# Products by zero weights, a longer share for ScalarE and eight banks in a four-layer network kernel

## The chip, the cores and the metric

The kernel runs on one core of a Trainium2 chip. The metric is the device time of one execution in microseconds. Before the change it is 7317.06 us, the median of three runs (7311.98 to 7319.36).

A core has a matrix engine (TensorE, PE in the profile; its weight loads are PEld), a vector engine (VectorE, DVE), an activation engine (ScalarE, ACT), a general one (GpSimd, POOL) and a queue engine that here issues nearly all DMAs (SyncE, SP). Each engine works through its own instruction stream in order; they meet through semaphores. TensorE writes its sums to PSUM, which has eight banks of 128 x 512 fp32.

## The reference

The input x has shape (16, 32, 128, 128). Four layers follow each other, each x = x + f(normalised x):

1. a row recurrence: `g = xt + W1_prev·shift(h) + W1_cur·h + b`, gates by sigmoid and tanh, 128 steps;
2. an 8-bit difference layer over 3x3 patches of 32 channels: `out = -sum |patch - w|`, with quantised x and w. This is the one the change mostly concerns: 288 differences for each output of each of 32 channels;
3. a Hartley transform of which 32 x 32 modes are mixed over channels and transformed back;
4. a small U-shaped network: five fixed edge operators, each normalised, then conv1, pool, conv2, pool, conv3, pool, conv4, then three times an upsampling deconvolution and a convolution (conv5, conv6, conv7), and `x * y`.

## The kernel before

**First stage** (`stage0`): statistics and the recurrence, up to about 880 us. The change doesn't touch it.

**The unit loop** (`Differences.run`): layer 2. A unit is half an image: 16 images, two halves, 32 units. Partitions hold four row blocks of 32 channels (for the evaluations, four copies: four output channels of a group by 32 input channels). `|a - w|` is written as `2·max(a - w, 0) - (a - w)`; the second part is linear and done by TensorE alone (`linear`, L601, nine taps). For the first, a unit has 72 evaluations, i = 0 to 71: tap i % 9 of output channels 4·(i // 9) to +3. An evaluation reads the tile q (66 rows of 130, fp16) and writes a tile d of 128 x 8192 or 8320 fp16. It is made either by VectorE (L684, `d_dve`, three buffers) or by ScalarE as a Relu with bias (L681, `d_act`, two buffers). TensorE then adds each tile over input channels into the unit's four banks `acc1`: `sums` (L586), 16 products of 128 x 512 with a 128 x 32 weight (`sel16`), each of which sums into one 32-partition block of a bank. After 72 tiles `finish` evicts the banks on VectorE (L567, then statistics, L569) and stores x2. The four banks are the only ones of this pool, so the next unit's sums cannot begin before L567 has emptied them.

**The account.** The order of everything in the loop is written out by the kernel when it is built. It keeps an account with a time for each engine (`weave.dve`, `weave.act`, `weave.pe`), with fixed prices: `DVE_US = 2.36` for an evaluation on VectorE, `ACT_US = 7.15` on ScalarE, `PE_US = 1.0` for a tile's sums. It gives an evaluation to ScalarE where by the account this ends no more than 0.5 us after VectorE would (and not from i = 68 on), and it takes the tiles' sums in the order in which the tiles end. All sums of a unit, those of ScalarE's last tiles too, stand before the next unit's first evaluation. When two VectorE tiles of the next unit stand in the order, the old unit's `finish` follows and the new banks are taken.

**The interleaved work** (`After`, a generator). Layers 3 and 4 of images already finished, in groups of four images: group 0 to 2 in a `Weave`. After each evaluation `weave.advance(due)` takes steps of this work as long as the account has TensorE free before the next tile ends. Its stages are `forward` (L1030), `mixing` (L1096), `back` (L1159, L1204, evicted by L1182, L1184), `statistics` (L1292), `conv1` (L1607), the small layers (L1455 for conv2 to conv4, L822 and L847 for the composed upsampling convolutions) and `last` (L822, L1735, L1698, L1708, store L1714). It has four banks of its own (pool `b_ps`). `spread` (L1543 on VectorE, L1546 on ScalarE) moves results with a bias, 16 pieces at a time, to the next padded tile.

**The tail** (`drain`). When the loop ends, the four `acc1` banks are given to a second weave, `end`, for group 3 alone (pool `c_ps`). `drain` takes steps of both weaves by turns, by their accounts, until both are done. In the profile the tail begins at 5942 us; group 2's last stores are issued at 7048, and from then group 3 is alone with its four banks.

Of the kernel before, what the change touches and what calls it, by code (L numbers as in the profile page):

```python
# [7 lines left out]
F32 = mybir.dt.float32  # L8
F16 = mybir.dt.float16
# [6 lines left out]
B, C, H, W = 16, 32, 128, 128  # L16
# [283 lines left out]
class Weave:  # L300
# [10 lines left out]
    def __init__(self, work):  # L311
        self.work, self.pending = work, None
        self.pe = self.dve = self.act = self.now = self.base = 0.0
        self.until = self.ready = 0.0
        self.draining = False
        self.finished, self.count, self.put_off, self.for_act, self.ends = -1, 0, [], [], {}

    def later(self, us, step):
# [19 lines left out]
    def run(self, v):  # L338
        (self.put_off if v in self.put_off else self.for_act).remove(v)
        dve, act = self.dve, self.act  # L340
        v[2]()
        self.ends[v[1]] = max([t for t, before in ((self.dve, dve), (self.act, act)) if t > before] + [0.0])
# [60 lines left out]
def drain(*weaves):  # L403

    live = list(weaves)
    for w in live:
        w.draining = True
    while live:
        w = min(live, key=lambda w: w.now)
        us = w.step()  # L410
        w.now = max(w.now + (us or 0.0), w.until)
        w.due(float("inf") if us is None else w.now)
        if us is None:
            live.remove(w)


def keep_order(nc, tc, start):
# [13 lines left out]


DVE_US, ACT_US, PE_US = 2.36, 7.15, 1.0
SLACK, CLOCK = 3.0, 1.0
SUMMED = ("summed",)


def rest(nc, tc, cst, sel16, bias, m1, r1, a, d, out):


    with ExitStack() as ctx:
        sm = ctx.enter_context(tc.tile_pool(name="s1_sm", bufs=1))
        stat = sm.tile([128, B, 8, 6], F32, name="stat2")
        with tc.tile_pool(name="s1_ps0", bufs=2, space=PSUM) as ps:
            first = Differences(nc, sm, ps, cst, sel16, m1, r1, a["adder_w"], d, stat)
        bg = ctx.enter_context(tc.tile_pool(name="b_ps", bufs=4, space=PSUM))
        after = After(nc, tc, "left", sm, bg, cst, bias, a, d, stat, out)
        weave = after.weave = Weave(after.work(range(NG - 1)))
        start = len(nc.cur_bb.bb.instructions)
        with ExitStack() as front:  # L450
            first.run(tc, front, weave)
        keep_order(nc, tc, start)

        end = copy.copy(after)
        end.side, end.ps = "right", ctx.enter_context(tc.tile_pool(name="c_ps", bufs=4, space=PSUM))
        end.weave = Weave(end.work([NG - 1]))
        end.weave.now = end.weave.base = weave.now
        end.weave.finished = B - 1
        drain(weave, end.weave)


class Differences:
# [10 lines left out]
    def __init__(self, nc, sm, ps, cst, sel16, m1, r1, w, d, stat):  # L473
# [32 lines left out]
        for j in range(4):  # L506
# [4 lines left out]
                start=True,  # L511
# [2 lines left out]
        nc.vector.tensor_scalar(sumw, p[:, :1], 2.0**-7, None, ALU.mult)  # L514
        self.r128, self.shift, self.qw, self.neg, self.sumw = r128, shift, qw, neg, sumw

        self.ring = [sm.tile([128, 8, P], F16, name=f"qt{i}") for i in range(2)]
        for t in self.ring:
            nc.gpsimd.memset(t, 0.0)
# [40 lines left out]
            self.nc.sync.dma_start(xr[i], jc_rows(self.d["x1"], b, half, 8 * i, 8))  # L560
        return xr

    def finish(self, b, half, acc, xr):
        nc = self.nc
        v = [xr[k // 2][:, 512 * (k % 2) : 512 * (k % 2) + 512] for k in range(4)]
        for k in range(4):
            nc.vector.scalar_tensor_tensor(v[k], acc[k], self.sumw, v[k], ALU.subtract, ALU.add)  # L567
        for k in range(4):
            nc.vector.bn_stats(self.stat[:, b, 4 * half + k, :], v[k])  # L569

        def store():
            for i in range(2):
                nc.sync.dma_start(jc_rows(self.d["x2"], b, half, 8 * i, 8), xr[i])
            if half:
                self.weave.finished = b

        start = max(self.weave.dve, self.weave.pe)
        self.weave.pe, self.weave.dve = start + 2.6, start + 5.6
        self.weave.later(max(self.weave.dve - self.weave.base, 0.0) + 0.5, store)
# [14 lines left out]
    def linear(self, acc, q, tap):  # L594
# [12 lines left out]
                )  # L607
        self.weave.pe = max(self.weave.pe, self.weave.now) + 0.45

    def run(self, tc, ctx, weave):  # L610
        nc, R, P = self.nc, self.R, self.P
        self.weave = weave
# [5 lines left out]
        with tc.tile_pool(name="s1_x0", bufs=4, side="right") as pool:  # L618
            xq = [self.unquantised(0, i, pool) for i in range(4)]
            for i in range(4):  # L620
                self.scaled(0, xq[i])
                self.quantise(0, i, xq[i])
                weave.due(float("inf"))
        before, following = None, self.loaded(0, 0)

        free, count = {True: [0.0] * 2, False: [0.0] * 3}, {True: 0, False: 0}
        for b in range(B):
            for half in range(2):
                q, acc = following, None
                late, xq, summed = [], {}, 0  # L630

                def sums(until, last):

                    nonlocal summed
                    while late and (min(late)[0] <= until or last):
                        end, n, act, t = min(late)
                        late.remove((end, n, act, t))
                        self.sums(acc, t, n, not summed, last and not late)
                        summed += 1
                        weave.pe = max(weave.pe, end + 0.2) + PE_US  # L640
                        free[act].append(weave.pe)

                for i in range(72):
                    if not acc and sum(not v[2] for v in late) == 2:

                        if before:
                            self.finish(*before)
                        acc = [ps.tile([128, 512], F32, name="acc1") for _ in range(4)]
                        sums(weave.dve, False)
                    if i % 4 == 0 and 24 <= i < 60:  # L650
                        self.linear(acc, q, i // 4 - 6)
                    if i == 8 and (b, half) != (B - 1, 1):
                        following = self.loaded(b + half, 1 - half)
                    if i == 40:
                        xr = self.residual(b, half)
                    if half == 0 and b + 1 < B:
                        k = (i - 6) // 15
                        if 0 <= k < 4 and (i - 6) % 15 == 0:
# [11 lines left out]
                        for act in (True, False)  # L670
                        if count[act] < len(free[act])
                    }
                    act = False not in ends or (True in ends and i < 68 and ends[True] <= ends[False] + 0.5)
                    t = dp.tile([128, R, P], F16, name="d_act" if act else "d_dve", bufs=2 if act else 3)

                    src = q[:, kh : kh + R, :] if kw == 1 else q[:, kh : kh + R, kw : kw + W]
                    dst = t if kw == 1 else t[:, :, :W]
                    late.append((ends[act], i, act, t))
                    count[act] += 1
                    if act:  # L680
                        nc.scalar.activation(dst, src, AF.Relu, bias=self.neg[:, i : i + 1])  # L681
# [1 line left out]
                    else:  # L683
                        nc.vector.tensor_scalar(dst, src, self.qw[:, i : i + 1], 0.0, ALU.subtract, ALU.max)  # L684
                        weave.dve = ends[act]
                    if acc and (not act or i == 71):
                        sums(weave.dve, i == 71)
                    made = sum(not v[2] for v in late)
                    if acc:
                        weave.advance(min([v[0] for v in late] + [weave.dve + DVE_US]))  # L690
                    else:
                        weave.advance(weave.dve + (2 - made) * DVE_US + (2.6 if before else 0.0))
                before = b, half, acc, xr
        self.finish(*before)
        weave.due(float("inf"))


# [178 lines left out]
class After:  # L876


    def __init__(self, nc, tc, side, sm, ps, cst, bias, a, d, stat, out):
        self.nc, self.tc, self.side, self.ps, self.cst, self.bias = nc, tc, side, ps, cst, bias  # L880
        self.a, self.d, self.stat, self.out = a, d, stat, out
        store = [d["up"][i] for i in range(3)]
        self.up5 = Composed(nc, sm, a, "deconv1", "conv5", bias[:, 7:8], bias[:, 4:5], store[0])
        self.up6 = Composed(nc, sm, a, "deconv2", "conv6", bias[:, 8:9], bias[:, 5:6], store[1])
        self.up7 = Composed(nc, sm, a, "deconv3", "conv7", bias[:, 9:10], bias[:, 6:7], store[2])
# [16 lines left out]
                    yield from self.last(g)  # L902

    def acc(self):
        return self.ps.tile([128, 512], F32, name="acc")

    def prepare(self):

# [627 lines left out]
    def spread(self, dst, src, blk, b, engine):  # L1536

        nc, weave = self.nc, self.weave
        for j in range(4):
            d, s = dst(slice(32 * blk, 32 * blk + 32), j), src[32 * j : 32 * j + 32]  # L1540
            bj = b[32 * j : 32 * j + 32]
            if engine is nc.vector:
                nc.vector.tensor_scalar(d, s, bj, None, ALU.add)  # L1543
                weave.dve += 0.3
            else:
                nc.scalar.activation(d, s, AF.Identity, bias=bj)  # L1546
                weave.act += 0.45
# [115 lines left out]
    def last(self, g):  # L1663

        nc, tc, cst, weave = self.nc, self.tc, self.cst, self.weave
        with self.pool("l_y") as yp, self.pool("l_x", 2) as xp:
# [39 lines left out]
            def done(x, unit):  # L1706
                for blk in range(4):
                    nc.scalar.activation(x[:, blk], x[:, blk], AF.Identity, bias=mean[:, blk : blk + 1])  # L1708
                weave.act += 4.4
                following[unit] = weave.later(14.0, lambda: store(x, unit))  # L1710

            def store(x, unit):
                for j in range(4):
# [200 lines left out]
```

## Time and profile before

| what | value |
|---|---|
| median of three runs | 7317.06 us |
| the profiled execution | 7308.39 us, span 7306.6 |
| instructions | 258155 |
| first stage | 0 to 880 us |
| unit loop, first to last evaluation | 920 to 5942 us |
| evaluations on VectorE, ScalarE | 1705, 599 |
| tail, two groups | 5942 to about 7056 us |
| tail, group 3 alone | about 7056 to 7307 us |
| granted TensorE clock, mean | 0.867 |

```profile
PE 5566.3 (76%) x121132; PEld 3000.3 (41%) x121132; DVE 5855.4 (80%) x7046; ACT 5318.0 (73%) x3116; POOL 36.3 (0%) x31
...
PE   4778566666677687998777676999788777798887
...
DVE  7787599999999999999898889999899982423232
ACT  2556399989999998998988878999898941131312
...
PEclk9899788888888898998888887999887876799996
```

The first line gives busy time, share of the span and instructions of each engine. The rows below cut the span in 40 slices; a digit is the busy share in tenths, and PEclk is the clock that TensorE was granted, in tenths of full speed. Slices 6 to 32 are the unit loop.

### The profile page before, as it was taken

To read this page: it belongs to the slowest core of one execution; us is meant where nothing else is said; L and a number is where in the kernel's file an instruction comes from. 1 tells how busy PE (TensorE), PEld (TensorE's weight loads), DVE (VectorE), ACT (ScalarE), POOL (GpSimd) and SP (SyncE) were. 2 spreads that over 40 slices of the span, in tenths; PEclk is the share of its full clock that TensorE was granted. 3 is DMA by queue.
4 is the path that set the end of the run, shared out by engine and by line. 5 is a ranking of instruction groups with operands and counts; after the bars stand their busy time and mean duration, and the time that the engine had idled before them with its cause. 6 is when DMAs were issued, how large, how long until landed. Compare 5 with 4: busy or idle time off the path is not lost. (4 is left out here: it accounts for less than half of the span.)

```text
span 7306.6 us, 258155 instructions
## 1 busy us (share of the span) xinstructions
PE 5566.3 (76%) x121132; PEld 3000.3 (41%) x121132; DVE 5855.4 (80%) x7046; ACT 5318.0 (73%) x3116; POOL 36.3 (0%) x31
## 2 busy tenths in 40 slices
PE   4778566666677687998777676999788777798887
PEld 3665322222244343333344333333334456445544
DVE  7787599999999999999898889999899982423232
ACT  2556399989999998998988878999898941131312
POOL 0000000000000000000000000000000000000000
PEclk9899788888888898998888887999887876799996
DMA  8654111111133442211342243111233245531324
GB/s 312 227 195 164 65 63 55 48 58 51 40 96 106 136 115 78 62 43 50 78 134 94 79 139 111 58 55 50 57 100 100 98 138 151 156 102 46 81 62 96
DMA packets 374268, 721.67 MB, mean 99 GB/s; under 512 B 50896, under 2 KB 219856, under 8 KB 362320
## 3 DMA queue, kind: packets, MB, share of 16 engines
q1 hardware_dynamic: 372768, 704.58, 31.3%
q8 instruction: 948, 15.53, 0.9%
q14 instruction: 120, 0.98, 0.0%
q10 hardware_dynamic: 432, 0.57, 0.0%
HBM read 507.21 MB, written 164.32 MB: 92 GB/s over the span
## 5 line engine op out<-in xcount | busy, mean ns | idle before, releaser
L681 ACT ACTIVATE d_act<-q,neg 128x8192 f16<-128x8192 f16 (+1 forms) x599 | 4237.0, 7141 | 383.8 <-PE acc L586 330.8
L684 DVE TENSOR_SCALAR d_dve<-q,qw 128x8192 f16<-128x8192 f16 (+1 forms) x1705 | 3929.7, 2360 | 187.4 <-PE acc L586 144.1
L586 PE MATMUL acc<-d_dve,sel 128*32 128x512 f16 x27280 | 1957.5, 415 | 750.4 <-DVE d_dve L684 741.5
L586 PEld LDWEIGHTS <-sel 128*32 128x32 f16 x36864 | 1045.7, 103 | 2521.4 <-issue 1862.7
L1607 PE MATMUL acc<-xp,wf 32*32 32x512 f32 x25600 | 1052.9, 625 | 50.7 <-issue 29.9
L586 PE MATMUL acc<-d_act,sel 128*32 128x512 f16 x9584 | 759.4, 439 | 346.2 <-ACT d_act L681 276.9
L1607 PEld LDWEIGHTS acc<-xp,wf 32*32 32x32 f32 x25600 | 415.9, 105 | 428.5 <-issue 344.9
L1252 ACT ACTIVATE xp<-xp,shift,stats 128x1280 f32<-128x1280 f32 (+1 forms) x128 | 182.5, 1434 | 434.5 <-DMA xp<-x_d 298.3
L1546 ACT ACTIVATE y<-pooled,b 32x128 f32<-32x128 f32 x512 | 204.7, 400 | 398.8 <-DVE pooled L1532 392.1
L207 PE MATMUL pg<-h,wb 64*64 64x20 f32 (+15 forms) x4096 | 393.7, 318 | 105.0 <-DVE h L256 64.0
L822 PE MATMUL acc<-y,u_conv 32*32 32x256 f32 (+1 forms) x9728 | 409.9, 491 | 82.6 <-issue 41.0
L244 ACT ACTIVATE gt<-pg,bias 128x20 f32<-128x20 f32 (+15 forms) x1024 | 316.6, 375 | 78.8 <-PE pg L207 72.0
L207 PE MATMUL pg<-e,wb 64*64 64x20 f32 (+15 forms) x4096 | 351.1, 313 | 17.2 <-DVE e L260 6.0
L207 PEld LDWEIGHTS pg<-h,wb 64*64 64x64 f32 x4096 | 245.4, 152 | 140.9 <-DVE h L256 90.5
L207 PE MATMUL pg<-xn,wb 64*64 64x28 f32 (+61 forms) x4096 | 283.9, 302 | 11.6 <-ACT gt L244 3.9
L822 PEld LDWEIGHTS acc<-y,u_conv 32*32 32x32 f32 x9728 | 193.8, 115 | 233.3 <-issue 152.8
L207 PEld LDWEIGHTS pg<-e,wb 64*64 64x64 f32 x4096 | 249.3, 154 | 93.0 <-DVE e L260 63.9
L1292 PE MATMUL acc<-xp 32*64 32x204 f32 (+3 forms) x8576 | 245.6, 351 | 31.5 <-ACT xp L1258 23.4
L255 ACT ACTIVATE th<-c 128x20 f32<-128x20 f32 (+15 forms) x256 | 81.3, 320 | 236.1 <-DVE c L253 234.5
L1735 DVE TENSOR_SCALAR s<-acc,l_ms,l_one 128x512 f32<-128x512 f32 x128 | 102.7, 829 | 168.8 <-PE acc L822 168.8
L207 PEld LDWEIGHTS pg<-xn,wb 64*64 64x64 f32 x4096 | 216.0, 153 | 36.6 <-ACT gt L244 10.9
L1292 PEld LDWEIGHTS acc<-xp 32*64 32x64 f32 (+1 forms) x8576 | 173.3, 137 | 123.5 <-issue 93.3
(203 smaller groups left out, 4173.4 us busy)
## 6 DMA issues: line engine op xcount, KB each, us to landing
xr<-x_d SPq DMA_DIRECT2D x192, 512.0 KB
xp<-x_d SPq DMA_DIRECT2D x112, 640.0 KB
q<-q_d SPq DMA_DIRECT2D x32, 2145.0 KB
x_d<-xr SPq DMA_DIRECT2D x128, 512.0 KB
x_in<-in_x_dram SPq DMA_DIRECT2D x16, 2048.0 KB
res<-in_x_dram SPq DMA_DIRECT2D x64, 512.0 KB
xn<-in_xs_dram SPq DMA_DIRECT2D x64, 512.0 KB
xn<-xn SPq DMA_DIRECT2D x128, 256.0 KB
```

What stands on the lines that cost most here:

```text
L207: nc.tensor.matmul(bank[c][q][64 * pair : 64 * pair + 64, :, :width], wb[half, 4 * kind + KIND[q]].rearrange("p b o -> p (b o)"), v[half], ...
L244: nc.scalar.activation(gt[:, q, :, :n], bank[c][q][:, :, :n], AF.Tanh if q == G else AF.Sigmoid, bias=bias[:, KIND[q] : KIND[q] + 1],)
L255: nc.scalar.activation(th[:, :, :n], cell, AF.Tanh)
L586: self.nc.tensor.matmul(acc[k][32 * j : 32 * j + 32, :], self.sel16[:, i // 9, :], d[:, row : row + 4, c : c + W], start=first, stop=last,)
L681: nc.scalar.activation(dst, src, AF.Relu, bias=self.neg[:, i : i + 1])
L684: nc.vector.tensor_scalar(dst, src, self.qw[:, i : i + 1], 0.0, ALU.subtract, ALU.max)
L822: nc.tensor.matmul(acc[blk][32 * j : 32 * j + 32, o : o + rows * n], t[part, 4 * par + tap, :], src[part, top : top + rows, left : left + ...
L1252: nc.scalar.activation(v, v, AF.Identity, bias=self.shift3, scale=self.stats3[:, 1])
L1292: nc.tensor.matmul(gram[blk][j : j + width, at : at + n], xp[part, l, 2 + j : 2 + j + width], xp[part, rows, j : j + width + 4], start=sta ...
L1546: nc.scalar.activation(d, s, AF.Identity, bias=bj)
L1607: nc.tensor.matmul(acc[blk][32 * j : 32 * j + 32, :], tap_of("all", tap)[rows], xp[rows, 4 * j + kh : 4 * j + kh + 4, kw : kw + W], start= ...
L1735: nc.vector.tensor_scalar(s.rearrange("p r w b -> p b r w"), acc[blk].rearrange("p (b r w) -> p b r w", b=2, w=64), istd[:, blk : blk + 1] ...
```

## The change

Four things change.

- **Filler.** A tile `zero` of 128 x 32 zeros is added. After `advance`, where the account still has TensorE idle before the next tile ends, `keep_busy` issues up to four packets of four products with these weights, on rows of q, into the unit's own banks with accumulation: they add zero. A packet is put down as 0.25 us. Nothing is issued before a unit's first sum.
- **ScalarE up to a unit's end.** The limit i < 68 is replaced by a bound: in the last four evaluations ScalarE may take one that ends up to `(71 - i) * DVE_US + LATE` after VectorE's next would, `LATE = 1.5`. A unit's sums are now kept with the unit; those still open at its end are issued during the first evaluations of the next one, all of them ahead of `finish`.
- **Eight banks for the last group.** When one weave of the tail is done, the other is told that it is alone. From then `acc` takes banks by fours from its own pool and from the first weave's pool in turn.
- **Also when alone**, `spread` gives blocks 0 and 2 to VectorE and 1 and 3 to ScalarE instead of all to one of them, and the store of a finished unit of `last` is placed 4 us instead of 14 us of the account after its last step.

```diff
+LATE = 1.5
...
+        end.spare = bg
...
+        self.zero = sm.tile([128, 32], F16, name="zero")
+        nc.vector.memset(self.zero, 0.0)
...
+    def keep_busy(self, acc, q, until):
...
+        start = max(self.weave.pe, self.weave.now)
+        for k in range(min(int((until - start - 0.1) / 0.25), 4)):
+            for j in range(4):
+                self.nc.tensor.matmul(
+                    acc[k][32 * j : 32 * j + 32, :], self.zero, q[:, :4, :W], start=False, stop=False
+                )
+            self.weave.pe = start + 0.25 * (k + 1)
...
+        def sums(unit, until, last=False):
...
+            late = unit["late"]
+            while late and (min(late)[0] <= until or last):
+                end, n, act, t = min(late)
+                late.remove((end, n, act, t))
+                self.sums(unit["acc"], t, n, unit["summed"] == 0, unit["summed"] == 71)
+                unit["summed"] += 1
+                weave.pe = max(weave.pe, end + 0.2) + PE_US
+                free[act].append(weave.pe)
...
-                        if before:
-                            self.finish(*before)
+                        if before:
+                            sums(before, weave.dve, True)
+                            self.finish(**before)
...
-                    act = False not in ends or (True in ends and i < 68 and ends[True] <= ends[False] + 0.5)
+                    act = False not in ends or (
+                        True in ends and ends[True] <= ends[False] + (0.5 if i < 68 else (71 - i) * DVE_US + LATE)
+                    )
...
-                    if acc and (not act or i == 71):
-                        sums(weave.dve, i == 71)
-                    made = sum(not v[2] for v in late)
-                    if acc:
-                        weave.advance(min([v[0] for v in late] + [weave.dve + DVE_US]))
+                    current = unit if unit["acc"] else before
+                    if current and not act:
+                        sums(current, weave.dve)
+                    due = [v[0] for v in current["late"]] if current else []
+                    if unit["acc"]:
+                        due.append(weave.dve + DVE_US)
                     else:
-                        weave.advance(weave.dve + (2 - made) * DVE_US + (2.6 if before else 0.0))
+                        made = sum(not v[2] for v in unit["late"])
+                        due.append(weave.dve + (2 - made) * DVE_US + (2.6 if before else 0.0))
+                    weave.advance(min(due))
+                    if unit["acc"] and 0 < unit["summed"] < 71:
+                        self.keep_busy(unit["acc"], q, min(due))
...
     def acc(self):
-        return self.ps.tile([128, 512], F32, name="acc")
...
+        self.banks += 1
+        ps = self.spare if self.weave.alone and self.banks // 4 % 2 else self.ps
+        return ps.tile([128, 512], F32, name="acc")
...
-            if engine is nc.vector:
+            if blk % 2 == 0 if weave.alone else engine is nc.vector:
...
-                following[unit] = weave.later(14.0, lambda: store(x, unit))
+                following[unit] = weave.later(4.0 if weave.alone else 14.0, lambda: store(x, unit))
```

## The prediction

> **What bounds the kernel now.** I read the page first, then the busy time by stretches, the waits of each engine, a timeline of one unit's end, and the chain of waits for the end. The profiled execution took 7308.4 us (span 7306.6), 8.7 under the median of the runs, 7317.1; the sum is made on the profiled one and shifted by 8.7.
>
> ```profile
> L681 ACT ACTIVATE d_act<-q,neg 128x8192 f16<-128x8192 f16 (+1 forms) x599 | 4237.0, 7141 | 383.8 <-PE acc L586 330.8
> L684 DVE TENSOR_SCALAR d_dve<-q,qw 128x8192 f16<-128x8192 f16 (+1 forms) x1705 | 3929.7, 2360 | 187.4 <-PE acc L586 144.1
> ```
>
> The 2304 evaluations (32 units of 72) go to two engines. VectorE's overlap a little, so one costs its busy time over its count: 3929.7/1705 = 2.305 us. ScalarE's costs 7.14. These lines also show who waits: both for TensorE's sums (L586), ScalarE longer.
>
> ```profile
> 920.00:5942.00 5022.00, 3854.22 (x78058) 1799.89 (x78061) 4735.17 (x3735) 4588.63 (x1211) 28.82 (x15) 0.88 0.26 79
> 1100.00:2000.00 900.00, 579.00 (x8376) 237.16 (x8376) 892.39 (x705) 842.18 (x130) 6.34 (x2) 0.86 0.14 51
> 2900.00:3300.00 400.00, 389.23 (x8748) 147.38 (x8748) 381.94 (x256) 377.29 (x198) 0.21 (x1) 0.99 0.17 51
> ```
>
> Columns: length, then busy TensorE products, weight loads, VectorE, ScalarE, GpSimd, then TensorE's clock. The first row is the whole unit loop: VectorE idles 287 of 5022 us, ScalarE 433, TensorE 1168. VectorE sets the time, ScalarE is close behind. The second row is a stretch with little interleaved work: VectorE is 99% busy although the clock is 0.86. The third has much interleaved TensorE work: 97% busy, clock 0.99. So the clock follows TensorE's load, and where VectorE is full it costs nothing.
>
> ```profile
> DVE d_dve L684 <- PE acc L586: 144.1, 88, 26.7
> DVE d_dve L684 <- DMA q<-q_d: 41.2, 1, 41.2
> ...
> 1618.24 21.35 ACT L681 ACTIVATE d_act<-q,neg 128x8320 f16<-128x8320 f16 x3
> 1647.96 21.15 ACT L681 ACTIVATE d_act<-q,neg 128x8192 f16<-128x8192 f16 x3 [8.37 <-PE acc L586]
> ...
> 1644.46 2.72 DVE L567 SCALAR_TENSOR_TENSOR xr<-acc,sumw,xr 128x512 f32<-128x512 f32 x4
> ...
> 1645.26 4.30 PE L586 MATMUL acc<-d_act,sel 128*32 128x512 f16 x32 [3.29 <-DVE xr L567]
> ```
>
> First VectorE's waits (total, times, longest), then a unit's end. ScalarE's three evaluations from 1618 are the old unit's last and the new unit's first two. Both of its buffers are then full, and it stands 8.37 us until the old banks are evicted (L567) and its first new tile summed. Following its instructions through the units, 207 of the 330.8 us fall on this third evaluation of a unit, about 6.5 us a unit: nearly room for one more evaluation.
>
> **The change, part by part.**
>
> *ScalarE up to a unit's end.* The order built from the changed program has 622 ScalarE evaluations and 1682 on VectorE: 23 move. VectorE: 23 x 2.305 = **53 us** less, on the path. ScalarE: 23 x 7.14 = 164 us more, beside it: cover is the 207 us. Its loop load becomes 4589 + 164 = 4753; with the first load (47.8) and its waits for interleaved work (some 70) it could end the loop no earlier than 4871, 151 under today: the floor of the gain. VectorE's own floor is lower: 4735 - 53 + 41 = 4723, plus waits.
> The new wait: the old unit's last sum may now come from ScalarE after VectorE has gone on, and VectorE's eviction of the banks (L567), with the evaluations queued behind it, waits for it. In the trace ScalarE's last evaluation of a unit ends 7 to 21 us before VectorE's (mean about 14), so one more 7.1 us fits, less the 2.3 us that VectorE ends sooner; and VectorE has two evaluations of the next unit (4.6 us) ahead of the eviction. Per unit this costs between 0 and 3 us (ScalarE's account is true, VectorE's 2.36 is 0.055 too long, 2.9 us over 53 evaluations): 0 to 96 us. I take 10, by the mean slack.
>
> *Filler.* 7008 products, 1752 packets of four, in the form of L586 (128x512, f16, 32 columns). In the timeline two groups of sixteen start 0.86 us apart at full clock (1625.36, 1626.22) and 1.66 at half (3479.24, 3480.90), so four cost 0.21 or 0.42 us. At full clock that is 1752 x 0.21 = 370 us against 1168 idle, each packet put where the kernel's account leaves a gap. What does it buy? [...] The row: in 1100 to 2000 TensorE's waits for VectorE's tiles are 231.7 us in 201 (1.15 us each), and the clock is 0.86. [...] By the rows the share of busy time decides: cut into 3.4 us pieces, the clock record falls to 0.5 after pieces with under about 45% busy and returns after about 80%. The measurement decides: filler should lift the loop's clock from 0.88 to 0.95 or more. Whether products by zero count as load no row shows. Worth in time: at most all 144.1 us of VectorE's waits for sums plus some 20 in interleaved work. But the longest, 26.7 us, has another chain (a slow load of xp, ScalarE behind it, TensorE in order behind ScalarE), and so have others. Waits in which the clock is low and no such chain stands add to 30 to 45. Below zero: a late TensorE must work through filler first, priced under the rivals. I take **-30**.
>
> *Moved interleaved work.* By the order, 130 L1159 and 48 L1204 products pass from the loop to the tail, with VectorE's 8 L1182, 8 L1184, 4 L1171: 8 x 0.680 + 8 x 0.677 + 4 x 1.048 = **15 us** off VectorE in the loop. In the tail, by the chain's pieces: 186 L1159 in 3.11 us, 59 L1204 in 8.02, so 2.2 + 6.5 = **+9** on TensorE, 83% busy there. VectorE's 15 is hidden in the tail (38% busy); so are the four stores to x3 and four reloads (512 KB each) that these steps issue on SP: group 2 has more than 1000 us left there and ends 250 before group 3.
>
> *Eight banks, shared spreading, earlier store.* They act only once group 2's work has ended. Its last stores are issued at 7048; the new order's count of spreading on VectorE (8 fewer) fits a start two conv1 chunks before that work ends. So they reach the last 250 us.
>
> ```profile
> 7201.99 0.88 DVE s L1735
> 7202.88 0.65 DVE xr L1698
> 7203.53 0.73 DVE s L1735
> 7204.26 0.04 issue
> 7204.30 3.55 PE acc L822 x49
> ```
>
> The chain: TensorE cannot start the next round until VectorE has emptied the banks. Such links sum to 14 us over the eight rounds of the last convolution, 4.3 at conv2 (7079.5 to 7083.8), 3.0 at conv6, 2 before it: 23. With eight banks TensorE goes on. Halving the spreading (16 x 0.28 us on conv4, 16 x 0.50 on conv5) saves about 4. The last eviction stays, and so do the stalls the profile calls issue. Store 4 us after instead of 14: SP waits for ScalarE's last step there anyway, 0. Between 10 and 45 (clock 0.59 to 0.71 there, could rise); I take **-25**.
>
> Hidden: the zero tile's memset (before the loop); the next q load, which waits for the old unit's last reader, is issued eight evaluations into a unit, some 15 us, while that reader ends within about 5.
>
> Sum: -53 + 10 - 30 - 15 + 9 - 25 = **-104**: 7204 profiled, **7213** as median.
>
> **Rivals.**
> *A, filler without worth*: the clock stays (zeros are no load) or VectorE never waited for it; 99% busy at 0.86 speaks for it, the late waits against. 7213 + 30 = 7243.
> *B, filler harms, slower*: the clock stays low and filler stands in the order before real sums. The record has 173 low stretches in the loop, 7.0 us each. In lean phases a step lasts 1.83 us (132/72); at half clock a sum takes 1.7 and two to three packets 1.1: 0.96 late per step, 3.7 us per stretch. VectorE's three buffers cover 4.6 - 1.7 = 2.9; beyond that it stalls, 0.8 x 173 = 138 us. Time 7243 + 138 = 7381. It decides once a stretch outlasts three steps. Against: full TensorE raises its own clock.
> *C, ScalarE's last evaluation is the new wait*: 96 instead of 10: 7299.
> *D, everything pays*: loop at ScalarE's floor (-151), tail -36: 7130.
>
> **How the numbers follow.** Forecast 47%, A 18, D 15, C 12, B 8. The range takes D's end and C's: 7125 to 7300, leaving B and tails. No change means within 0.2%, 14.6 us. Faster: forecast, A, D and over half of C, 0.87; same 0.05; slower 0.08.
>
> **What would show it.** Clock in the loop 0.95 or more; ScalarE's wait for sums near 170 us from 330.8; L684 at 1682; the last evaluation's end near 5855 instead of 5942; after group 2's end about 225 us. I am wrong if VectorE waits long before L567 (C), if its L684 waits grow while the clock stays low (B), or if the loop ends at 5885 with the clock high (A).

## The result, and the profile after

The changed kernel takes **7215.2 us** (median of four, 7210.6 to 7221.0) against 7318.2 for the kernel before beside it (7312.0 to 7320.5): ratio **0.9861 [0.9844, 0.9878]**, 103 us less. The forecast was 7213. Its total holds; one of its terms does not, and most of what follows is about that one.

The profiled execution took 7210.55 us, span 7207.9 (before: 7306.6). The 98.7 us between the spans lie here, cut at VectorE's first and last evaluation and at the last conv1 product (L1638, before L1607):

| stretch | before, us | after, us | difference |
|---|---|---|---|
| up to the first evaluation | 920.3 | 921.2 | +1 |
| unit loop | 5020.6 | 4940.9 | -80 |
| VectorE busy in it | 4734 | 4671 | -63 |
| VectorE idle in it | 287 | 270 | -17 |
| tail, up to the last conv1 product | 1124.7 | 1127.0 | +2 |
| tail, from there to the end | 241.1 | 218.6 | -22 |

The page's costliest groups, after (line, engine, operation, shapes, count; then busy time, mean ns of one; then idle time ahead of them and what ended it):

```profile
L702 ACT ACTIVATE d_act<-q,neg 128x8192 f16<-128x8192 f16 (+1 forms) x622 | 4398.3, 7143 | 204.1 <-PE acc L592 154.9
L705 DVE TENSOR_SCALAR d_dve<-q,qw 128x8192 f16<-128x8192 f16 (+1 forms) x1682 | 3877.4, 2362 | 166.4 <-PE acc L592 124.1
...
L622 PE MATMUL acc<-q,zero 128*32 128x512 f16 x7008 | 503.0, 398 | 0.0
```

L702 and L705 are the old L681 and L684, and L592 is the old L586. The 23 evaluations have moved (622 and 1682), ScalarE's wait for sums fell from 330.8 to 154.9 us, VectorE's from 144.1 only to 124.1. L622 is the filler.

Busy time by stretches, after (start and end, length; busy PE, PEld, DVE, ACT, POOL, each with its count; granted TensorE clock; DMA share; GB/s):

```profile
921.00:5862.00 4941.00, 4074.06 (x84586) 1950.88 (x84589) 4670.90 (x3690) 4747.68 (x1234) 27.22 (x15) 0.91 0.26 80
1100.00:2000.00 900.00, 704.28 (x12194) 339.29 (x12196) 888.12 (x703) 876.48 (x136) 7.22 (x2) 0.95 0.14 52
2900.00:3300.00 400.00, 387.64 (x8412) 141.26 (x8415) 379.79 (x263) 393.42 (x200) 3.22 (x1) 0.97 0.18 57
```

In 1100 to 2000, where little is interleaved, the clock rose from 0.86 to 0.95, and VectorE was 99% busy before and is so after. Over the whole loop it rose from 0.88 to 0.91, not to 0.95.

VectorE's waits, after (total, times, longest):

```profile
DVE d_dve L705 <- PE acc L592: 124.1, 89, 12.4
...
DVE es_w L1383 <- DMA gm<-in_gram_dram: 33.0, 2, 21.9
...
DVE xr L573 <- PE acc L592: 15.6, 5, 4.3
```

The last is the new wait: `finish` (L573, before L567) stands for ScalarE's last sum, 15.6 us in all, 12.7 of it in the loop. The longest wait of an evaluation for sums is 12.4 us, where it was 26.7. The sum of all such rows inside the loop explains nearly all of the idle time's -17: evaluations' waits for sums -20, DMAs of the interleaved work -15 (86.5 to 71.2), the new wait +13, waits for interleaved TensorE work +6.

### The profile page after: what moved, and what is told of

It is laid out like the page before. It is cut to its first block, busy times and chain, and to the rows that moved or that the text cites. A ratio compares the mean times of both kernels' runs of the same rounds, so it can differ in the third digit from the quotient of the medians.

```text
span 7207.9 us, 272193 instructions
## 1 busy us (share of the span) xinstructions
PE 5763.4 (80%) x128140; PEld 3183.3 (44%) x128140; DVE 5804.1 (81%) x7016; ACT 5477.6 (76%) x3147; POOL 34.7 (0%) x31
## 5 line engine op out<-in xcount | busy, mean ns | idle before, releaser
L702 ACT ACTIVATE d_act<-q,neg 128x8192 f16<-128x8192 f16 (+1 forms) x622 | 4398.3, 7143 | 204.1 <-PE acc L592 154.9
L705 DVE TENSOR_SCALAR d_dve<-q,qw 128x8192 f16<-128x8192 f16 (+1 forms) x1682 | 3877.4, 2362 | 166.4 <-PE acc L592 124.1
L592 PE MATMUL acc<-d_dve,sel 128*32 128x512 f16 x26912 | 1882.1, 403 | 512.9 <-DVE d_dve L705 458.9
L592 PEld LDWEIGHTS <-sel 128*32 128x32 f16 x36864 | 1027.2, 100 | 2137.7 <-issue 1482.8
L1638 PE MATMUL acc<-xp,wf 32*32 32x512 f32 x25600 | 1034.2, 616 | 36.5 <-issue 26.7
L592 PE MATMUL acc<-d_act,sel 128*32 128x512 f16 x9952 | 732.2, 417 | 315.1 <-ACT d_act L702 306.5
L1638 PEld LDWEIGHTS acc<-xp,wf 32*32 32x32 f32 x25600 | 418.5, 104 | 397.0 <-issue 319.5
L622 PE MATMUL acc<-q,zero 128*32 128x512 f16 x7008 | 503.0, 398 | 0.0
L849 PE MATMUL acc<-y,u_conv 32*32 32x256 f32 (+1 forms) x9728 | 359.4, 466 | 69.7 <-issue 45.1
L622 PEld LDWEIGHTS <-zero 128*32 128x32 f16 x7008 | 211.9, 101 | 195.6 <-issue 40.5
L849 PEld LDWEIGHTS acc<-y,u_conv 32*32 32x32 f32 x9728 | 171.1, 111 | 193.1 <-issue 139.3
L1739 ACT ACTIVATE xr<-xr,l_ms 128x1024 f32<-128x1024 f32 x64 | 70.0, 1141 | 221.9 <-DVE xr L1729 199.3
```

The costliest lines, as they stand in the source:

```text
L592: self.nc.tensor.matmul(acc[k][32 * j : 32 * j + 32, :], self.sel16[:, i // 9, :], d[:, row : row + 4, c : c + W], start=first, stop=last,)
L622: self.nc.tensor.matmul(acc[k][32 * j : 32 * j + 32, :], self.zero, q[:, :4, :W], start=False, stop=False)
L849: nc.tensor.matmul(acc[blk][32 * j : 32 * j + 32, o : o + rows * n], t[part, 4 * par + tap, :], src[part, top : top + rows, left : left + ...
L1638: nc.tensor.matmul(acc[blk][32 * j : 32 * j + 32, :], tap_of("all", tap)[rows], xp[rows, 4 * j + kh : 4 * j + kh + 4, kw : kw + W], start= ...
```

## The experiments

Ratios are to the kernel before, run beside each on the same chip; its medians there were 7315.4 (the four kernels of the first part), 7304.5 (ghost_filler, free_filler, ghost_only, banks_only) and 7312.4 (the rest). Where times of different chips are subtracted, such differences of up to 11 us come in. Each kernel below is the changed one with the edit shown.

### One part taken away

`no_filler`: no products and none in the account.

```diff
-                    if unit["acc"] and 0 < unit["summed"] < 71:
-                        self.keep_busy(unit["acc"], q, min(due))
```

> The changed kernel without its filler; all else stays. By the built order 625 evaluations are ScalarE's (3 more than with filler) and nothing of group 2's back stage moves to the tail. Theory of the prediction: the clock in the loop falls back from 0.91 to about 0.88 and VectorE's waits return: +30 for the clock, +6 for the work that stays in the loop, -7 for the three evaluations: about 7244 us. Rival (filler without worth, VectorE is full at any clock): 7214 or less. Rival (filler in front of real sums harms): under 7205.

7269.99, 0.9940 [0.9928, 0.9952]: 55 us above the changed kernel, and above what any of the recorded theories said. So filler seemed worth even more than the 30 of the prediction.

`old_limit`: ScalarE's limit as before.

```diff
-                        True in ends and ends[True] <= ends[False] + (0.5 if i < 68 else (71 - i) * DVE_US + LATE)
+                        True in ends and i < 68 and ends[True] <= ends[False] + 0.5
```

> The changed kernel with the old limit i < 68 for ScalarE; 598 evaluations on ScalarE, 1706 on VectorE, 7120 filler products. Theory: 24 evaluations go back to VectorE, 24 x 2.305 = 55 us, less the 10 for the later eviction: about 7260 us, and ScalarE's wait for its third tile of a unit is back near 200 us. Rival (once the clock is up, ScalarE's wait is short anyway and VectorE has room): under 7235.

7285.12, 0.9960 [0.9948, 0.9972]: 70 us above. ScalarE's waits for sums come back, as its wait row shows:

```profile
ACT d_act L702 <- PE acc L592: 300.0, 50, 20.1
```

Of these 300 us, 203 fall on the third evaluation of a unit (before 207, after 35). That is the mechanism of the prediction. The loop is 75 us longer than the changed kernel's (5015.6 against 4940.9): 54 of it are VectorE's busy time (4726 instead of 4671), as forecast; the other 20 are idle time, since this edit changes the order as well.

`never_alone`: the last group keeps four banks, the old spreading and the old store.

```diff
-            for w in live:
-                w.alone = True
```

> The changed kernel in which the last group never learns that it is alone: four banks, old spreading, store after 14 us. The loop is the same instruction for instruction. Theory: +25, about 7240 us. Rivals: the end gains little since TensorE is the bound there at its low clock, +10, 7225; or the clock rises with eight banks and the end gains more than the waits, +45, 7260.

7248.2, 0.9916 [0.9904, 0.9928]: 33 us above. The loop has the same order and nearly the same length (4938.2), and the stretch from the last conv1 product to the end takes 252.6 us against 218.6.

`filler_only`: both of these edits, so that of the change filler alone is left.

> Only the filler: the changed kernel with the old limit i < 68 and never alone. Theory: 30 for the clock and 6 for the work moved to the tail under the kernel before: about 7282 us. Rival (filler without worth): 7312. Rival (harm): over 7318. If the filler's gain is there only with the moved evaluations, the gain here is smaller than what taking the filler out of the changed kernel costs.

7320.0, 1.0007 [0.9998, 1.0017]: worth nothing. The three removals add to 55 + 70 + 33 = 158 us (by the ratios 58 + 72 + 40 = 170), more than the 103 of the whole, and filler is worth 55 by one reading and 0 by another. The parts are not independent. What they share is the account: every packet booked in `weave.pe` makes `advance` place the interleaved steps elsewhere. So taking filler out takes out two things, the products and the order that their bookings make.

### The products apart from the order

`ghost_filler`: the packets are booked, but no product is issued. All other instructions stand in the changed kernel's order.

```diff
-            for j in range(4):
-                self.nc.tensor.matmul(
-                    acc[k][32 * j : 32 * j + 32, :], self.zero, q[:, :4, :W], start=False, stop=False
-                )
```

> The changed kernel in which the account still books the filler but no product is issued: on every engine the order of all other instructions is that of the changed kernel. Theory P (the products work, by the clock): the loop's clock falls to about 0.88 and the time goes to that without filler, about 7265 us, all of it in the loop. Theory O (what pays is the order into which the booked filler pushes the interleaved work): about 7215 us, as with the products.

`free_filler`: the products are issued, but not booked, so all else stands in no_filler's order.

```diff
-            self.weave.pe = start + 0.25 * (k + 1)
```

> The reverse: filler products are issued but not booked, so the order of all other instructions is that of the kernel without filler (7270 us), with 9216 filler products in it. Theory P: the clock rises above 0.91 and the time falls to 7215 to 7225 us. Theory O: it stays at 7265 to 7275 us. If products stand in the way of real sums it is slower than 7275.

`ghost_only`: filler_only's bookings without its products.

> Filler alone, as in the run that measured 7320 us, but booked only and not issued: old limit, never alone. Theory P with a loss by the order: the order by itself costs some 20 us that the products win back, about 7340 us. Theory O: the products do nothing, 7320 us. Theory N (without the moved evaluations VectorE's waits do not hang on the clock): 7320 us or less, though the clock falls to 0.88.

| order made by | products | ratio | loop, us | VectorE idle in it | clock in it |
|---|---|---|---|---|---|
| the changed kernel | 7008 | 0.9861 [0.9844, 0.9878] | 4940.9 | 270 | 0.91 |
| (ghost_filler) | 0 | 0.9850 [0.9836, 0.9863] | 4937.4 | 268 | 0.89 |
| no_filler | 0 | 0.9940 [0.9928, 0.9952] | 5007.9 | 327 | 0.88 |
| (free_filler) | 9216 | 0.9922 [0.9909, 0.9936] | 5005.4 | 325 | 0.92 |
| filler_only | 7120 | 1.0007 [0.9998, 1.0017] | 5009.9 | 285 | 0.91 |
| (ghost_only) | 0 | 1.0013 [1.0005, 1.0021] | 5021.7 | 294 | 0.88 |

Each pair has one order: in the traces the instructions of VectorE, ScalarE and SP follow each other in the loop in the same sequence. Within a pair the loop differs by 3.5, 2.5 and 11.8 us, the first time against the products. Between the first two orders it differs by 64 to 71. How far traces of one loop differ by themselves can be seen too: the changed kernel's loop with its products took 4940.9, 4938.2 (never_alone) and 4941.9 us (banks_only, on ghost_filler's chip), filler_only's 5009.9 and in old_limit 5015.6. So the first two differences are within this scatter, and the third is 6 to 12 us. By the ratios the products lose 8 us in the first pair and gain 13 and 4 in the others; in each pair the intervals overlap. (Free_filler's 7255.69 us lie between what the two theories said; of its 14 us under no_filler's median, 11 lie between the kernels before on the two chips, and its loop is only 2.5 us shorter.)

VectorE's waits for sums say the same, here for ghost_filler (124.1 with products):

```profile
DVE d_dve L701 <- PE acc L592: 123.4, 93, 12.8
```

for no_filler:

```profile
DVE d_dve L705 <- PE acc L592: 170.0, 103, 18.0
```

and for free_filler:

```profile
DVE d_dve L704 <- PE acc L592: 166.8, 101, 19.3
```

Filler_only and ghost_only:

```profile
DVE d_dve L703 <- PE acc L590: 130.2, 87, 8.7
DVE d_dve L699 <- PE acc L590: 142.0, 98, 7.4
```

With the products these waits are 3 us shorter in free_filler, 12 in filler_only (7 in old_limit, which has the same loop: 135.1), and no shorter in the changed kernel. The busy time by stretches shows why it is so little. No_filler in 1100 to 2000:

```profile
1100.00:2000.00 900.00, 574.44 (x8504) 242.00 (x8498) 888.60 (x703) 878.29 (x136) 6.30 (x2) 0.87 0.14 51
```

free_filler there:

```profile
1100.00:2000.00 900.00, 764.28 (x13468) 373.74 (x13471) 889.42 (x704) 878.23 (x135) 6.32 (x2) 0.96 0.14 52
```

The clock goes from 0.87 to 0.96, so products with zero weights do count as load, and VectorE is busy 888.6 and 889.4 of 900 us. In this stretch, where filler finds room, VectorE hardly waits for TensorE.

`late_12`: an order without filler, in which ScalarE may end at most 1.2 us later than VectorE instead of 1.5.

```diff
-LATE = 1.5
+LATE = 1.2
...
-                    if unit["acc"] and 0 < unit["summed"] < 71:
-                        self.keep_busy(unit["acc"], q, min(due))
```

> No filler and no booking at all, LATE 1.2 instead of 1.5: 621 evaluations on ScalarE instead of 625, another order of the interleaved work (of group 2's back stage 610 products in the tail instead of 512). Theory S (the order decides by where interleaved loads fall behind q loads, filler or not): the time differs from the 7270 us of LATE 1.5 by more than 15 us in either direction, though only four evaluations (9 us) move. Theory F (booked filler makes a better order as such): 7265 to 7285 us.

7206.94, 0.9858 [0.9844, 0.9871], with 621 evaluations on ScalarE instead of 622. Its loop by stretches:

```profile
920.00:5843.00 4923.00, 3782.06 (x77686) 1769.27 (x77689) 4672.11 (x3691) 4740.66 (x1233) 42.54 (x15) 0.89 0.26 80
```

Beside no_filler (0.9940, 625 evaluations on ScalarE) it gives ScalarE four evaluations fewer and moves what is interleaved, and gains some 60 us at nearly the same load of VectorE (4672 against 4681): its loop is 85 us shorter, its tail 22 longer. It is as fast as the changed kernel without a single product by zero. The intervals of the changed kernel, ghost_filler and late_12 overlap; none of them is shown to be the best.

### The end

`banks_only`: eight banks when alone, but the old spreading and the old store.

```diff
-            if blk % 2 == 0 if weave.alone else engine is nc.vector:
+            if engine is nc.vector:
...
-                following[unit] = weave.later(4.0 if weave.alone else 14.0, lambda: store(x, unit))
+                following[unit] = weave.later(14.0, lambda: store(x, unit))
```

> The changed kernel in which the last group, once alone, takes eight banks but spreads and stores as before. Loop unchanged. Theory: the banks are worth 23 to 29 of the 33 us that the three parts bring together, so about 7220 us. Rival: the halved spreading is the larger part, since the next stage waits for it: about 7235 us.

7212.86, 0.9862 [0.9849, 0.9876]: the changed kernel's ratio. The last stretch takes 225.6 us in its trace against 218.6, which the medians don't show. It had the changed kernel's loop with all products, and ran on the same chip as ghost_filler, which was 14 us faster; of these, 4.5 us are the loop in the traces and 8 the last stretch, in which the two differ as well. The last stretch by busy time, in never_alone (four banks):

```profile
6991.00:7243.00 252.00, 185.96 (x4799) 111.14 (x4781) 93.25 (x203) 51.77 (x68) 0.00 (x0) 0.70 0.36 83
```

and in banks_only (eight):

```profile
6987.00:7212.00 225.00, 142.72 (x4815) 89.43 (x4800) 92.77 (x203) 52.03 (x68) 0.00 (x0) 0.77 0.39 93
```

The counts agree; with eight banks the same products are busy 143 instead of 186 us, at a clock of 0.77 instead of 0.70. TensorE's wait for VectorE's evictions in never_alone, in this stretch:

```profile
PE acc L847 <- DVE s L1764: 7.5, 10, 0.9
```

and in the changed kernel:

```profile
PE acc L849 <- DVE s L1766: 1.2, 2, 0.8
```

In the kernel before (7065 to 7306) it was much as in never_alone:

```profile
PE acc L822 <- DVE s L1735: 6.9, 8, 1.3
```

The waits that eight banks remove are only 6 us of the 27 by which the stretch is shorter (252 to 225). The higher clock alone would bring 186 us to 169 (186 x 0.70/0.77), if busy time follows it; where the rest comes from, and why the clock is higher, no run shows. Nor does all the busy time saved reach the total: TensorE's idle time named issue grows from 21 us in never_alone to 39 in banks_only.

Old_limit and filler_only are a second pair of this kind, with the old limit: with all three parts of the end the last stretch takes 210.7 us, without them 253.1, and the medians are 35 us apart.

### What the order decides: DMAs behind the load of q

What remains of VectorE's idle time comes in a few long pieces. Of the two longest in the changed kernel (22.1 us for `xw`, 21.9 for `gm`) this is the second, in VectorE's timeline (start, duration, the instruction, the idle time ahead and its releaser):

```profile
4472.49 0.60 DVE L1383 TENSOR_TENSOR es_w<-acc,gm 128x420 f32<-128x420 f32 x1 [21.86 <-DMA gm<-in_gram_dram]
```

SP's timeline just before it:

```profile
4423.19 0.55 SPq L559 DMA_DIRECT2D q<-q_d  x1
4427.72 0.36 SPq L1277 DMA_DIRECT2D xp<-x_d  x1
4428.14 31.14 SPq L1435 DMA_DIRECT2D v<-fold_d  x3
4459.38 1.38 SPq L1389 DMA_DIRECT2D gm<-in_gram_dram  x2
```

And the stretches in and after SP's standstill:

```profile
4428.00:4436.00 8.00, 5.65 (x104) 2.63 (x93) 7.11 (x13) 8.00 (x2) 0.00 (x0) 1.00 0.69 113
4436.00:4459.00 23.00, 5.50 (x48) 1.99 (x48) 14.01 (x21) 23.00 (x4) 0.00 (x0) 0.54 0.27 68
4459.00:4464.00 5.00, 0.00 (x0) 0.00 (x0) 0.00 (x0) 1.44 (x1) 0.00 (x0) 0.50 0.95 160
```

SP stands 31 us in three issues of `v` (128 x 1440, fp32), nearly all of it in the first, 5 us after it has issued the next unit's q (2145 KB). For 23 of these 31 us the DMA engines are busy for about a quarter (0.27, 68 GB/s); then what was held back runs at 0.95. At 68 GB/s the 2145 KB of q would take 32 us, an estimate from this row, and as long as SP stands. The table `gm` (128 x 420) that VectorE needs is issued only at 4459. All eight single issues over 10 us in the changed kernel's loop come 2 to 26 us behind a q load; of ten before, nine do, and the tenth is a q load.

No_filler's longest stall, in VectorE's timeline, shows that SP need not stand for this:

```profile
4556.64 1.72 DVE L1448 SCALAR_TENSOR_TENSOR wf<-v,ops,wf 128x1440 f32<-128x1440 f32 x1 [30.81 <-DMA v<-fold_d]
```

SP's timeline before it:

```profile
4512.40 0.56 SPq L559 DMA_DIRECT2D q<-q_d  x1
4515.68 8.23 SPq L1433 DMA_DIRECT2D v<-fold_d  x3
```

These three issues take 0.32 us each; by the order of the three buffers VectorE waits for the first. Issued 3.3 us behind q, its data came 41 us later, and from 4520 to 4556 the DMA engines are busy for 0.43 (95 GB/s). So the load itself is late, whether SP stands or not.

Why the DMA share stays near a quarter behind this q load (0.25, 0.24 and 0.31 in the three pieces from 4436 to 4459), no run shows: the load was run in this one form alone.

If the q load in SP's queue were what holds back the others, it should help to issue it elsewhere. `after_q_act` does so from ScalarE's queue; `nofill_q_act` and `before_q_act` do the same in no_filler and in the kernel before.

```diff
-        self.nc.sync.dma_start(q, bass.AP(q_d.tensor, first, [[0, 4], [(H + 2) * P, C], [1, (self.R + 2) * P]]))
+        self.nc.scalar.dma_start(q, bass.AP(q_d.tensor, first, [[0, 4], [(H + 2) * P, C], [1, (self.R + 2) * P]]))
```

> The changed kernel with one edit: the load of q (2145 KB, one a unit) is issued from ScalarE's queue instead of SP's. All other instructions keep their order. Theory S: the long waits of VectorE's queue for interleaved loads (es_w 21.9, xw 22.1, d_dve 12.4 us behind a late load) come from SP standing in its next DMA issues (14 to 35 us) behind the q load; with q elsewhere they go, about 50 us: 7165 us. Rival B: the bytes take the same engines, a load beside q is as late as one behind it: 7205 to 7220. Rival I: ScalarE pays 1 to 2 us of issue 32 times and is nearly full: 7215 or more.

> The kernel without filler and without its booking (7270 us), with the q load from ScalarE's queue. Theory S: this order of the interleaved work meets more of SP's stalls (wf 30.8, d_dve 18.0 and 14.5, xm 12.2), so it gains more than the changed kernel does: 7190 us, and the gap of 55 us between the two orders closes to 25 or less. Rival B or I: 7255 to 7270, the gap stays.

> The kernel before with the q load from ScalarE's queue. Theory S: xm 21.7, xr 22.6 and d_dve 26.7 go in part: some 50 us, about 7265 us; the difference to the changed kernel with the same edit is then near the sum of what is left of it (moved evaluations and end), about 100 us. Rival B or I: 7300 to 7320.

7524.35, 7580.78 and 7591.55: 1.0292 [1.0278, 1.0306], 1.0366 [1.0350, 1.0381] and 1.0383 [1.0368, 1.0397]. All three are slower by 210 to 280 us than the kernel before, which none of the recorded theories allowed for. ScalarE's wait row of after_q_act, for the loop, shows where:

```profile
ACT xq L540 <- DMA xq<-x_d: 297.4, 13, 31.2
```

In the changed kernel this row is 12.2 us. The three loops are 305, 300 and 281 us longer than with the load on SP's queue, and ScalarE waits 285, 276 and 289 us more for `xq`. One of the thirteen, in ScalarE's timeline:

```profile
1195.38 0.51 ACTq L559 DMA_DIRECT2D q<-q_d  x1
...
1246.53 1.24 ACT L540 ACTIVATE xq<-xq,shift,r 128x1024 f32<-128x1024 f32 x1 [19.69 <-DMA xq<-x_d]
```

and in SP's:

```profile
1202.00 0.54 SPq L536 DMA_DIRECT2D xq<-x_d  x1
```

From ScalarE's queue the q load is issued 6.6 us ahead of a 512 KB load for which ScalarE itself waits. That one now lands 44 us after its issue, and ScalarE's evaluations stand behind it. In the changed kernel SP issues it at this place 2.3 us ahead of q's load, and ScalarE does not wait. In the loop of after_q_act SP still has 13 issues of over 10 us (303 us together), and 11 of them come within 27 us behind a q load, although this is now on another queue. So what is issued behind a q load comes late on another queue than the q load's as well (44 us here), SP's queue is not where the delay arises, and my simple account of it is refuted. A q load on ScalarE's queue that is issued behind `xq` was not tried.

## Why the prediction was right, and where it was wrong

- **ScalarE up to a unit's end: right.** -53 on VectorE is in its busy time (-63 together with the moved back work's -10). Old_limit returns 54. The new wait at `finish` cost 13 in the loop where 10 were taken. ScalarE's last evaluation of a unit ended 13.8 us before VectorE's on average before the change and ends 0.8 us before it now, and in 10 of 32 units after it. So the mean slack is all but gone, where the prediction's own sum (14 less 7.1 and 2.3) had left 4.6, but rival C's 96 us did not come.
- **Filler: the step that failed.** The -30 rested on waits of VectorE for sums at low clock. The clock did rise, but at a fixed order the products make the loop between 3.5 us longer and 11.8 us shorter (by the ratios between a loss of 8 and a gain of 13, no pair clear of noise). The 30 to 45 us of waits that I had put down to the clock are not removed by it in the changed kernel: 124.1 with products, 123.4 without. A worth of 0, as rival A had it, came nearer in time, and by the second of A's two reasons: the clock didn't stay (0.86 before and 0.95 after in 1100 to 2000; the last section has the gaps ahead of its falls), but that gains hardly any time, because VectorE, 99% busy there, hardly waits for TensorE.
- **What stood in for it: the order.** VectorE's idle time apart from the new wait fell by 30 us (-17 - 13), by chance the number forecast. Since the pairs show that the products don't make it, what is left is where the interleaved work stands: the 26.7 us stall for sums is gone, and DMA stalls are 15 us less. This change of order comes from the new limit and from the bookings together: the bookings alone (ghost_only) leave VectorE's idle time at 294 us, where it was 287. I had treated the order only as a count of steps moved between loop and tail. Over the five orders of the loop that were run with q's load on SP, VectorE idles between 251 us (late_12) and 327 (no_filler): 76 us, more than any term of the sum. A forecast would have had to follow the changed order to each DMA stall, which I did not do.
- **Moved interleaved work: -10 in the loop and +2 in the tail** where -15 and +9 were taken: together -8 against -6. That this fits is in part luck: in the traces 352 products of L1159 and 96 of L1204 more run behind the last evaluation, where the prediction had counted 130 and 48, so that at its own prices the tail should have paid 19. No run took this step alone; no_filler, in which none of these products passes to the tail, has a tail 5.6 us shorter than the changed kernel's.
- **Eight banks: right in size** (-22.5 in the trace against -25), half right in reason. With four banks the last stretch took 241.1 us in the kernel before, but 252.6 in never_alone and 253.1 in filler_only, so that the fit is in part chance: at an equal order the end is worth 33 to 35 us by the medians. I had 23 us of waits for evictions, 14 of them in the last convolution; TensorE's own idle time there was 6.9, and 1.4 at conv2 where I had 4.3. I had added up whole links of the chain, during which TensorE was in part still busy. The larger part of the gain came with fewer busy microseconds at a higher clock, which I had noted only as "could rise". Of the shared spreading and the earlier store no run shows a gain in the median.
- **The marks.** 1682 evaluations, ScalarE's wait (154.9 for 170) and the end (218.6 from the last conv1 product, for 225 from group 2's end) came about as said, the loop's end at 5862 for 5855; the clock of 0.95 in the loop did not come. Rival A (filler without worth) was right about filler and wrong about the time, because it left the order alone. B is excluded by the pairs: with products the loop is at most 4.5 us longer (banks_only against ghost_filler).

What makes one order better than another is open beyond the stalls shown. No run repairs a single stall in an order.

## What to carry to other kernels

Where a built-in account decides the order of instructions, any edit that books time in it changes two things; separate them by booking without issuing and by issuing without booking, before the effect is put down to the instructions. Removals from such a kernel don't add up (158 for 103 here), and a small change of a constant can be worth as much as a feature. Before an engine's clock is raised, look at who waits for it in the stretch in question: an engine that is 99% busy there, as VectorE was, has next to nothing to gain.

## What the runs showed of the hardware

- Products with zero weights raise the granted clock: 0.87 to 0.96 in 1100 to 2000, with 13468 products instead of 8504 (no_filler and free_filler).
- The clock record of the two traces (before and after the change) has two levels, full and half, and its stretches (462 before, 354 after) are all but the last of each record whole multiples of 3.41 us long. Cut into pieces of that length, TensorE's busy share in a piece goes with what follows. In the loop of the kernel before, all 115 full-clock pieces with under 42% busy were followed by half clock, but only 34 of the 951 with over 50%; of the half-clock pieces none of the 128 with under 75% was followed by full clock, and 174 of the 220 with over 78% were. In the changed kernel's loop it is 82 of 82 and none of 81. At the 49 falls between 1100 and 2000 before the change, the longest idle gap of TensorE that reaches into the piece ahead of the fall is 1.2 to 4.7 us, 1.9 in the median.
- The products of the last group kept TensorE busy for 186 us with four banks (never_alone, 4799 of them) and for 143 with eight (banks_only, 4815), at a clock of 0.70 and 0.77.
- A 512 KB load issued 6.6 us behind the 2145 KB load of q landed 44 us after its issue, although the two came from different engines' queues (after_q_act); a load of `v` issued 3.3 us behind q on the same queue came after 41 us (no_filler). That move of the q load made the three kernels 3.8 to 4.4% slower than with the load on SP's queue (by the ratios).
